# Another order of TensorE's matmuls between the two layers of a CIN kernel (f32, one Trainium2 core)

## The chip, the cores and the metric

The kernel runs on one core of one Trainium2 chip (trn2). The metric is the device time of one execution in microseconds; for a version of the kernel it is the median of several runs. A profile is one further execution, recorded by the hardware profiler, whose own time stands beside it. In the profile PE is TensorE (matmuls), PEld its weight loads, DVE VectorE, ACT ScalarE, POOL GpSimd and SP SyncE (here only DMA issues).

## The reference

Two layers of a compressed interaction network over x of shape 4096 rows x 32 fields x 16 embedding values, all in f32:

```python
def _cin_layer(out, x, W, b, gamma, beta):
    r, _, e = x.shape
    h = jnp.einsum('rne,rfe->rnfe', out, x).reshape(r, -1, e)
    h = jnp.einsum('rce,oc->roe', h, W) + b[None, :, None]
    return _batchnorm(h, gamma, beta)      # over rows and embedding values
h1 = _cin_layer(x, x, W1, b1, g1, beta1)
out, direct1 = (h1[:, :64], h1[:, 64:])
direct2 = _cin_layer(out, x, W2, b2, g2, beta2)
return jnp.concatenate([direct1, direct2], axis=1).sum(axis=-1)
```

Layer 1 has 128 output channels. The first 64 (here "kept") feed layer 2; the other 64 ("direct") are only normalized and summed. The batch norm needs the mean and variance of a channel over all 65,536 sites (row x embedding value), so layer 2 can't begin before the last kept channel of the last site is known.

## The kernel before

**Layer 1** goes over 128 tiles of 512 sites (`T`). DVE forms the products of pairs of fields as `z` (L365), PE multiplies them by W1: four matmuls per tile with a contraction of 128 rows (L397), and one with 32 rows for the field pairs at distance d = 16, whose products stand in `zr` for eight tiles at once (L358). ACT evicts each PSUM bank three times: for the statistics, for the kept half (to `h`, stored in DRAM) and for the direct half (`ed`). DVE's `bn_stats` collects the statistics.

**The last four tiles** (`ENDING`, k = 0 to 3) are done in column halves from L423 on, so that the kept channels of all four are ready first. A phase (`direct` = 0 for kept, 1 for direct) multiplies by only 64 columns of W1. Two tiles' halves stand in different column halves of the array and run side by side: tile k writes the half `(k + direct) % 2` of its own bank. Each bank thus takes a kept half in the first phase and a direct half, on the other 64 partitions, in the second. `begin_halves` (L438) issues the four d = 16 matmuls of a phase, one for each tile on its own 32 rows of the array; they open the accumulation in their banks. `add_halves` (L428) adds the main products of two tiles, four matmuls each, alternating between the tiles.

In the kept phase (L458 to L471) ACT evicts the two kept halves of a chunk of two tiles (L468), DVE takes their statistics (L470), and the chunk is stored. Then a short chain on DVE and ACT (`ScaleShift`, L474 to L479) makes the scale and shift of the 64 kept channels, and L484 makes `blocks` from them. A small matmul with `spread` (L502) spreads these to the layout that layer 2 multiplies in, DVE copies the result from PSUM to `keep` (L503).

In the direct phase (L494 to L516) PE's order is: the four d = 16 matmuls, the main products of tiles 0 and 1, the first main product of tiles 2 and 3, the spreading matmul, the other three main products of tiles 2 and 3. ACT evicts the direct halves of tiles 0 and 1 (L511) right after; those of tiles 2 and 3 are put off into layer 2 (`late_evictions`).

**Layer 2** goes over 64 chunks of 2 x 512 sites, each in four stages. In a stage ACT turns a loaded part of `h` into a factor `f` (L630, scaled and shifted by `keep`), DVE multiplies it with x into `zz` (L643 for the very first stage, in four parts, L638 for the others), POOL forms sums of these (L674, L677, L685), and PE multiplies by combinations of W2 (L669). The field products come in a scheme with fewer multiplications, hence the sums.

**What sets the order.** Nothing is planned by cost. From L423 on, every instruction of PE, DVE, ACT and POOL goes through `queue` (L226), which chains it behind the one before it on its engine: an engine's instructions start in the order in which the Python code makes them. Waits between engines follow from who writes and reads a tile. A matmul into a bank half that opens an accumulation waits until ACT has evicted what stood in that bank. All of these matmuls are recorded under L426 (where `matmul` issues them), all factors under L630 (where `act` does).

Of the kernel before, what the change touches and what calls it, by code (L numbers as in the profile page):

```python
# [68 lines left out]
def tile_cin(ctx: ExitStack, tc: tile.TileContext, xa, xb, xr, w1, w1m, w2, bn, out):  # L69
# [156 lines left out]
    def queue(engine, make):  # L226

        with tc.issue_after(lasts[engine].ins) if engine in lasts else nullcontext():
            lasts[engine] = make()
        return lasts[engine]  # L230
# [4 lines left out]
    begun = factors.tile([P, T], FP, tag="f", name="begun")  # L235
# [25 lines left out]
    with ExitStack() as one:  # L261
# [23 lines left out]
        w1_sb = wpool.tile([P, 6, P], FP, tag="w1", name="w1_sb")  # L285
# [62 lines left out]
        def leftovers(r):  # L348
            zr = rpool.tile([P, T], FP, tag="zr", name="zr")
            nc.vector.tensor_tensor(zr, r[:, :T], r[:, T:], ALU.mult)  # L350
            return zr
# [23 lines left out]
        for t in range(NT - ENDING):  # L375
# [5 lines left out]
            if s == 0 and t > 0:  # L381
                zr = leftovers(r)
# [5 lines left out]
            if t == 0:  # L388
                with tc.issue_after(product.ins):
                    zr = leftovers(r)  # L390
# [32 lines left out]
        half_of = (low, high)  # L423

        def matmul(ps, w, z, start, stop):
            queue("pe", lambda: nc.tensor.matmul(ps, w, z, start=start, stop=stop))  # L426

        def add_halves(banks, zs, direct, ks, ms):  # L428

            for m in ms:  # L430
                for k in ks:
                    matmul(
                        banks[k][half_of[(k + direct) % 2]],
                        w1_sb[:, m, half_of[direct]],
                        zs[k][:, m // 2, m % 2, :],
                        False,
                        m == 3,
                    )  # L438

        def begin_halves(banks, zr, direct):  # L440

            for k in range(ENDING):
                rows = slice(32 * k, 32 * (k + 1))
                to = banks[k][half_of[(k + direct) % 2]]
                matmul(to, w1_sb[rows, 5, half_of[direct]], zr[rows, :], True, False)

        zs = []
        for k in range(ENDING):
# [5 lines left out]
        with tc.issue_after(lasts["dve"].ins):  # L454
            for t in (ending - 2, ending - 1):
                evicted = finish(t)
        banks = [psum.tile([P, T], FP, tag="ps", name="ps") for _ in range(ENDING)]
        begin_halves(banks, zr, 0)  # L458
        for c in range(NC - ENDING // 2, NC):
            ks = tuple(2 * c + half - ending for half in range(2))  # L460
            add_halves(banks, zs, 0, ks, range(4))
            h = opool.tile([KEEP, 2 * T], FP, tag="h", name="kept")
            for half, k in enumerate(ks):
                at = half_of[half]
                to = h[:, half * T : (half + 1) * T]
                bias = (b1, b1_swapped)[half][at]
                with tc.issue_after(evicted.ins):
                    queue("act", lambda: nc.scalar.activation(to, banks[k][at], AF.Identity, bias=bias))  # L468
                stats = stats1.more[low, 2 * k : 2 * k + 2].rearrange("p a b -> p (a b)")
                queue("dve", lambda: nc.vector.bn_stats(stats, to))  # L470
            nc.scalar.dma_start(hs[c], h)  # L471
# [19 lines left out]
        keep_ps = factors.tile([P, 4, 2], FP, tag="f", name="keep_ps")  # L491
        keep = const.tile([P, 4, 2], FP, tag="keep", name="keep")

        begin_halves(banks, zr, 1)  # L494
        for c in range(NC - ENDING // 2, NC):
            eds[c] = epool.tile([P, T], FP, tag="ed", name="ed")
            ks = tuple(2 * c + half - ending for half in range(2))
            if c < NC - 1:
                add_halves(banks, zs, 1, ks, range(4))
            else:  # L500
                add_halves(banks, zs, 1, ks, range(1))
                matmul(keep_ps, spread, blocks, True, True)  # L502
                queue("dve", lambda: nc.vector.tensor_copy(keep, keep_ps))  # L503
                add_halves(banks, zs, 1, ks, range(1, 4))
            for half, k in enumerate(ks):
                at = half_of[1 - half]
                bias = (b1, b1_swapped)[half][at]
                to = eds[c][half_of[half]]

                def evict(to=to, at=at, bias=bias, k=k):  # L510
                    return nc.scalar.activation(to, banks[k][at], AF.Identity, bias=bias)  # L511

                if c < NC - 1:
                    queue("act", evict)
                else:
                    late_evictions.append(evict)  # L516

    direct = const.tile([P, 2], FP, tag="direct", name="direct")
# [463 lines left out]
```

## Time and profile before

| | us |
|---|---|
| median of 5 runs | 2092.37 |
| lowest and highest of them | 2091.89, 2095.96 |
| the profiled execution | 2093.71 |
| its span, first to last instruction | 2091.6 |
| granted PE clock over the span | 0.996 |
| first matmul of layer 1, of the kept phase, of the direct phase | 9.82, 475.05, 483.08 |
| spreading matmul | 492.26 |
| first matmul of layer 2, last one | 496.15, about 2074 |

The times in the lower rows are counted from the first instruction of the profiled execution. A row of the time line reads: start, duration, engine, line, operation, output<-inputs, shape, how many were merged; in brackets, how long the engine had been idle and what released it. PE's rows merge instructions that overlap, so a duration spans the whole group. One f32 matmul shows as two passes, each with its own weight load; so `x8` in a row of PE are four matmuls. `128*64` means a contraction of 128 rows and 64 output columns. An engine that waits at the head of its queue holds all that stands behind.

### The profile page before, as it was taken

The page shows a single profiled execution, that of the slowest core. Times are in us where ns is not written, and L with a number is a line of the kernel's source. Part 1 is how long each engine was busy: PE and PEld are TensorE (multiplying, and loading weights), DVE is VectorE, ACT ScalarE, POOL GpSimd, SP SyncE. Part 2 cuts the span into 40 slices and gives each one's busy share as a digit, 9 for nine tenths or more (in the row PEclk, how much of TensorE's full clock was granted, in tenths as well). Part 3 has the DMA queues.
Part 4 walks back from the last instruction along what each step waited for, and adds up shares of the span by engine and source line. Part 5 has one row for each costly group of instructions (what it writes and reads, how often), then busy time and mean ns, then how long its engine had stood idle before and what let it go on. Part 6 is the DMA issues. An engine that isn't in the chain of part 4 may idle for free.

```text
span 2091.6 us, 23628 instructions
## 1 busy us (share of the span) xinstructions
PE 2069.3 (99%) x8634; PEld 1029.6 (49%) x8634; DVE 1890.5 (90%) x1391; ACT 1007.9 (48%) x1594; POOL 1471.7 (70%) x453
## 2 busy tenths in 40 slices
PE   9999999999999999999999999999999999999996
PEld 3444444443443555555555555555555555555553
DVE  8998888887999999999999998999999989999996
ACT  4555555554454444444444445454444454444443
POOL 0000000003899999999999999999999999999995
PEclk9999999999999999999999999999999999999998
DMA  9999999996766687777676777766677777767751
GB/s 385 378 347 349 333 359 354 347 337 178 174 162 171 162 195 188 193 175 173 162 191 166 183 176 176 173 172 162 171 167 186 173 174 176 171 163 169 171 142 41
DMA packets 112020, 440.65 MB, mean 211 GB/s; under 512 B 13088, under 2 KB 13088, under 8 KB 103456
## 3 DMA queue, kind: packets, MB, share of 16 engines
q1 hardware_dynamic: 105456, 418.43, 73.2%
q10 hardware_dynamic: 6448, 20.72, 2.6%
q8 instruction: 67, 1.10, 0.2%
q14 instruction: 49, 0.40, 0.1%
HBM read 417.07 MB, written 22.02 MB: 210 GB/s over the span
## 4 chain that ended last, share of the span: by engine, by line
PE 94%; DVE 2%; POOL 1%; issue 1%; ACT 1%; DMA 1%; DVEq 0%; SPq 0%; ACTq 0%; POOLq 0%
PE x L669 72%; PE ps L397 21%; PE ps L358 2%; DVE zz L638 1%; POOL t L677 0%; DMA h<-kept 0%; POOL t L674 0%; PE ps L426 0%; DMA b<-in_xb 0%; ACT f L630 0%; DVE zz L643 0%; DVE e L633 0%; ACT both L630 0%; DVE z L365 0%; DVE d L912 0%
## 5 line engine op out<-in xcount | busy, mean ns | idle before, releaser
L669 PE MATMUL x<-zz,s_sb 128*64 128x512 f32 x2048 | 946.8, 592 | 1.0 <-PE ps L426 0.8
L669 PE MATMUL x<-zz,w_sb 128*64 128x512 f32 x2312 | 890.3, 593 | 0.0
L677 POOL TENSOR_TENSOR t<-zz,t 128x2048 f32<-128x2048 f32 x191 | 870.8, 4559 | 15.0
L669 PE MATMUL x<-t,s_sb 128*64 128x512 f32 x1528 | 694.2, 593 | 0.1
L630 ACT ACTIVATE f<-a,keep 128x512 f32<-128x512 f32 x512 | 398.1, 778 | 415.2 <-DVE zz L638 373.1
L638 DVE TENSOR_TENSOR zz<-f,b 128x2048 f32<-128x2048 f32 x255 | 580.6, 2277 | 0.1
L638 DVE TENSOR_TENSOR zz<-f,bx 128x2048 f32<-128x2048 f32 x255 | 579.8, 2274 | 0.0
L674 POOL TENSOR_TENSOR t<-zz 128x1024 f32<-128x1024 f32 x191 | 453.1, 2372 | 89.8 <-DVE zz L638 80.1
L685 POOL TENSOR_TENSOR th<-zz,th 128x1024 f32<-128x1024 f32 x64 | 151.9, 2374 | 490.7 <-DVE th L633 490.7
L397 PE MATMUL ps<-z,w_sb 128*128 128x512 f32 x992 | 434.3, 596 | 1.3 <-DVE z L365 1.3
L669 PEld LDWEIGHTS x<-zz,s_sb 128*64 128x64 f32 x2048 | 280.1, 137 | 227.1 <-issue 163.5
L669 PEld LDWEIGHTS x<-zz,w_sb 128*64 128x64 f32 x2312 | 306.8, 137 | 168.1 <-issue 88.6
L669 PE MATMUL x<-t,w_sb 128*64 128x512 f32 x764 | 360.9, 595 | 0.9 <-POOL t L677 0.9
L365 DVE TENSOR_TENSOR z<-a,b 128x2048 f32<-128x2048 f32 (+1 forms) x129 | 293.7, 2278 | 54.3 <-PE ps L397 43.8
L669 PEld LDWEIGHTS x<-t,s_sb 128*64 128x64 f32 x1528 | 206.6, 137 | 223.8 <-issue 182.0
L397 PEld LDWEIGHTS ps<-z,w_sb 128*128 128x128 f32 x992 | 186.2, 190 | 247.2 <-issue 239.1
L329 ACT ACTIVATE e<-ps,bn_sb 128x512 f32<-128x512 f32 x124 | 85.2, 687 | 224.2 <-PE ps L397 205.0
L630 ACT ACTIVATE u<-e,bn_sb 64x512 f32<-64x512 f32 x64 | 46.3, 723 | 218.9 <-DVE e L633 218.9
L669 PE MATMUL x<-th,s_sb 128*64 128x512 f32 x256 | 130.8, 592 | 0.0
L633 DVE TENSOR_TENSOR both<-both,x 128x512 f32<-128x512 f32 x64 | 44.0, 688 | 94.6 <-ACT both L630 94.6
L669 PEld LDWEIGHTS x<-t,w_sb 128*64 128x64 f32 x764 | 101.9, 137 | 54.3 <-issue 18.9
L669 PE MATMUL x<-zz,neg_sb 128*64 128x512 f32 x264 | 124.1, 592 | 0.0
(104 smaller groups left out, 1233.1 us busy)
## 6 DMA issues: line engine op xcount, KB each, us to landing
a<-h SPq DMA_DIRECT2D x256, 512.0 KB, 5.7
a<-in_xa SPq DMA_DIRECT2D x128, 512.0 KB, 6.4
b<-in_xb SPq DMA_DIRECT2D x128, 512.0 KB, 7.4
b<-in_xb SPq DMA_DIRECT2D x64, 1024.0 KB, 8.8
bx<-in_xb SPq DMA_DIRECT2D x64, 512.0 KB, 7.8
bx<-x SPq DMA_DIRECT2D x64, 512.0 KB, 9.4
h<-kept ACTq DMA_DIRECT2D x64, 256.0 KB, 5.6
r<-in_xr SPq DMA_DIRECT2D x16, 512.0 KB, 7.6
```

Source lines behind the costliest of these rows:

```text
L329: nc.scalar.activation(e, ps, AF.Identity, bias=b1)
L358: nc.tensor.matmul(pss[t + k], w1_sb[rows, 4 + t % GROUP // 4, :], zr[rows, :], start=not ended, stop=ended)
L365: return nc.vector.tensor_tensor(z[:, k], a.rearrange("p (a t) -> p a t", a=2)[:, k].unsqueeze(2).to_broadcast([P, n, 2, T]), b.rearrange( ...
L397: nc.tensor.matmul(pss[t], w1_sb[:, m, :], z[:, m // 2, m % 2, :], start=(t == m == 0), stop=(t > 0 and m == 3))
L630: return queue("act", lambda: nc.scalar.activation(to, source, AF.Identity, **scale_bias))
L633: return dve(lambda: nc.vector.tensor_tensor(to, x, y, ALU.add))
L638: dve(lambda: nc.vector.tensor_tensor(z, a, b.rearrange("p (k q) t -> p k q t", k=2), ALU.mult))
L669: queue("pe", lambda: nc.tensor.matmul(self.of[x], w, b, start=start, stop=stop))
L674: queue("pool", lambda: nc.gpsimd.tensor_tensor(t[:, 0], z[:, 1], z[:, 0], ALU.add))
L677: queue("pool", lambda: nc.gpsimd.tensor_tensor(t[:, 1:3], z[:, 2:4], twice, ALU.subtract))
L685: queue("pool", lambda: nc.gpsimd.tensor_tensor(t[:, 1:3, 0], z[:, 2:4, 1], twice, ALU.subtract))
```

## The change

Only the order of PE's matmuls in the direct phase changes, with the marks that open (`start`) and end (`stop`) the accumulation in each bank. Before, the d = 16 matmuls of all four tiles came first and opened it. Now the main products of tiles 0 and 1 come first and open their banks; then come the four d = 16 matmuls, which end the accumulation of tiles 0 and 1 and open that of tiles 2 and 3; then the spreading matmul; then all main products of tiles 2 and 3. The kept phase is as it was. `begin_halves` is now `add_leftovers_halves`.

```diff
-        def add_halves(banks, zs, direct, ks, ms):
-
-            for m in ms:
+        def add_halves(banks, zs, direct, ks, begun, ended):
+
+            for m in range(4):
                 for k in ks:
                     matmul(
                         banks[k][half_of[(k + direct) % 2]],
                         w1_sb[:, m, half_of[direct]],
                         zs[k][:, m // 2, m % 2, :],
-                        False,
-                        m == 3,
+                        m == 0 and not begun,
+                        m == 3 and ended,
                     )
 
-        def begin_halves(banks, zr, direct):
+        def add_leftovers_halves(banks, zr, direct, begun):
 
             for k in range(ENDING):
                 rows = slice(32 * k, 32 * (k + 1))
                 to = banks[k][half_of[(k + direct) % 2]]
-                matmul(to, w1_sb[rows, 5, half_of[direct]], zr[rows, :], True, False)
+                matmul(to, w1_sb[rows, 5, half_of[direct]], zr[rows, :], k not in begun, k in begun)
...
-        begin_halves(banks, zr, 0)
+        add_leftovers_halves(banks, zr, 0, ())
         for c in range(NC - ENDING // 2, NC):
             ks = tuple(2 * c + half - ending for half in range(2))
-            add_halves(banks, zs, 0, ks, range(4))
+            add_halves(banks, zs, 0, ks, True, True)
...
-        begin_halves(banks, zr, 1)
         for c in range(NC - ENDING // 2, NC):
             eds[c] = epool.tile([P, T], FP, tag="ed", name="ed")
             ks = tuple(2 * c + half - ending for half in range(2))
             if c < NC - 1:
-                add_halves(banks, zs, 1, ks, range(4))
-            else:
-                add_halves(banks, zs, 1, ks, range(1))
+
+                add_halves(banks, zs, 1, ks, False, False)
+                add_leftovers_halves(banks, zr, 1, ks)
                 matmul(keep_ps, spread, blocks, True, True)
                 queue("dve", lambda: nc.vector.tensor_copy(keep, keep_ps))
-                add_halves(banks, zs, 1, ks, range(1, 4))
+            else:
+                add_halves(banks, zs, 1, ks, True, True)
```

## The prediction

> **What bounds the kernel now.** I read the page first, then the busy time by stages, then the rows of TensorE (PE) around the change, then those of ScalarE (ACT) and VectorE (DVE) there.
>
> ```profile
> span 2091.6 us, 23628 instructions
> PE 2069.3 (99%) x8634; PEld 1029.6 (49%) x8634; DVE 1890.5 (90%) x1391; ACT 1007.9 (48%) x1594; POOL 1471.7 (70%) x453
> ```
>
> PE is busy for 99% of the span. Time is saved either by shortening PE's work or by taking out one of its few stalls. The stages show where those are (columns: stretch, its length, busy time of PE, PEld, DVE, ACT and POOL, then granted clock, DMA share, GB/s):
>
> ```profile
> 482.68:486.09 3.41, 3.10 (x12) 0.56 (x8) 1.59 (x3) 1.36 (x2) 0.00 (x0) 1.00 0.60 215
> 486.09:489.51 3.42, 3.42 (x9) 1.01 (x10) 1.38 (x8) 0.59 (x2) 0.00 (x0) 0.50 0.35 77
> ...
> 492.92:496.33 3.41, 2.63 (x14) 0.79 (x12) 2.64 (x3) 1.45 (x2) 0.00 (x0) 1.00 0.19 30
> 496.33:572.45 76.12, 74.86 (x338) 31.45 (x336) 71.48 (x51) 35.51 (x58) 62.32 (x20) 1.00 0.70 170
> 572.45:2074.00 1501.55, 1501.55 (x6962) 793.46 (x6962) 1379.77 (x935) 719.32 (x1141) 1405.75 (x427) 1.00 0.70 169
> ```
>
> The reader is to see three things. From 572.45 to 2074 PE never stops: whatever moves the start of layer 2 moves the end. Between 496.33 and 572.45 PE lacks only 1.26 us. And from 486.09 to 489.51 its clock was granted at 0.50, after a window in which it was "busy" 3.10 of 3.41 us, but mostly with passes of 32 rows. The seam between the layers is therefore the place. Its PE rows (start, duration; one f32 matmul is two passes):
>
> ```profile
> 475.05 1.09 PE L426 MATMUL ps<-zr,w_sb 32*64 32x512 f32 x8
> ...
> 476.06 7.09 PE L426 MATMUL ps<-z,w_sb 128*64 128x512 f32 x32
> ...
> 484.46 1.79 PE L426 MATMUL ps<-zr,w_sb 32*64 32x512 f32 x4 [0.31 <-ACT kept L468]
> ...
> 486.18 6.14 PE L426 MATMUL ps<-z,w_sb 128*64 128x512 f32 x20
> ...
> 492.26 0.39 PE L426 MATMUL keep_ps<-blocks,spread 64*128 64x8 f32 x2
> ```
>
> The eight d = 16 passes of the kept phase take 1.01 us until the next work starts (475.05 to 476.06). The same eight in the direct phase take from 483.08 to 486.18, 3.10 us, since the last two tiles' matmuls wait for ACT to evict the kept halves of their banks. Who waits for whom after that:
>
> ```profile
> 484.43 0.68 ACT L468 ACTIVATE kept<-ps,b_swapped 64x512 f32<-64x512 f32 x1
> ...
> 487.68 0.16 DVE L484 TENSOR_TENSOR blocks<-block,ss 64x8 f32<-64x8 f32 x1
> ...
> 491.50 0.68 ACT L511 ACTIVATE ed<-ps,bn_sb 64x512 f32<-64x512 f32 x1 [4.44 <-PE ps L426]
> 492.21 0.68 ACT L511 ACTIVATE ed<-ps,b_swapped 64x512 f32<-64x512 f32 x1
> ...
> 492.68 0.17 DVE L503 COPY keep<-keep_ps 128x8 f32<-128x8 f32 x1 [4.84 <-PE keep_ps L426]
> ...
> 492.88 1.48 ACT L630 ACTIVATE f<-a,keep 128x512 f32<-128x512 f32 x2
> ...
> 493.69 1.23 DVE L643 TENSOR_TENSOR zz<-f,b 128x1024 f32<-128x1024 f32 x1 [0.85 <-ACT f L630]
> ```
>
> The factors that open layer 2 (`blocks`) are ready at 487.84, but their spreading matmul stands in PE's queue behind ten slots of main products and starts at 492.26. The first `f` needs `keep` (copied by 492.85) and ACT, which evicts two direct halves until 492.89. DVE's first `zz` starts at 493.69, the first matmul of layer 2 at 496.15.
>
> **The change part by part.** Nothing is added or removed on any engine: the same 16 main matmuls, four d = 16 matmuls and one spreading matmul, with other start and stop marks. The queues of ACT, DVE, POOL and SP keep their order, and no DMA issue moves past another. So the sum is one of waiting.
>
> *Main products first.* Two tiles' halves run side by side, so 16 passes are 8 slots. A slot is 0.43 us at full clock (7.09 us for 16 slots with the drain). The slot after the last kept one is due at 482.98 (the last issues at 482.55). Their banks 0 and 1 were evicted by 481.14, so nothing holds them. 482.98 + 8 x 0.43 = 486.42.
>
> *Then the four d = 16 matmuls.* Banks 2 and 3 are evicted by 485.11 (484.43 + 0.68), 1.3 us before they are asked for: the wait goes. They cost what they cost in the kept phase: 0.09 for the change of rows (such gaps lie at each change in layer 1), 1.09 to their end: 486.51 to 487.60. What hid nothing before hides now: the eviction lies beside main products.
>
> *Evictions, then f.* ACT starts the first direct eviction 0.04 after PE's end (491.46 to 491.50), the second 0.71 later, and `f` 0.67 after that: 487.64, 488.35, **489.02**.
>
> *The spreading matmul.* PE is free for it near 487.55 and waits for `blocks` until 487.84 + 0.05 (an ACT end to the waiting weight load: 484.41 to 484.46) = 487.89, a new wait of about 0.35 us. Queued behind it are the last 8 slots. It takes 0.39, the copy 0.04 + 0.17, so `keep` stands at 488.49 and `f` could start at 488.52. ACT is free only at 489.02, so the evictions, not the factors, end last. The bounds of this step: 488.52 if the evictions run earlier than I think, and later than 489.02 only if `blocks` slips by over 0.5 us. I take 489.02, from the nearer rows.
>
> *The last 8 slots* restart 0.31 after the spreading matmul (492.26 to 492.57): 488.20 + 3.44 + 0.17 drain = 491.8. With `f` 3.86 earlier the first matmul of layer 2 is due at 496.15 - 3.86 = 492.29, so they hide behind `f` and `zz` with 0.5 us to spare. The late evictions of banks 2 and 3 come on ACT at 499.21 - 3.86 = 495.35, long after.
>
> **The sum:** 492.88 - 489.02 = **3.86 us**. About 2.0 of it is the wait in the d = 16 block (3.10 against 1.01 plus 0.09), 1.7 the half clock: four slots of 0.86 in place of 0.43 after 486.18, which come only because the 32-row block fills a window. All that follows hangs on `f`, so it moves as one. By the profiled execution (2093.71 us, of which 2091.6 span) that makes 2089.85. That execution lies 1.34 above the median of the five runs, 2092.37. If the ordinary runs pay what the trace shows, their median goes to **2088.5**.
>
> [...]
>
> **The rivals.**
>
> *A, the gate was open in ordinary runs.* [...] For: the profiled run is 1.34 over the median, close to 1.7. Against: four of the five runs lie within 0.8 us, no two groups 1.7 apart. Then `keep` in before comes four half slots earlier (4 x 0.43 = 1.7) and the gain is 3.86 - 1.7 = 2.2: **2090.2**.
>
> *B, the start is earlier and the gain is lost before 572.* POOL's sums release PE at 572.45, and there PE lacks about 1 us; the loads of the second chunk wait for `f` too. Against: POOL's first sum waits for `zz`, and SP's loads from 494.39 for `f`, so both move along. If something fixed in time holds them, 0 to 1.3 us is left: about **2091.5**.
>
> *C, slower: the gate closes at the start of layer 2.* From 486.5 to 488.2 PE now has 32-row passes, a wait and 8-column passes. One closed window costs 3.41 / 2 = 1.7 on PE; the first is nearly covered (0.5 spare at 491.8, 1.26 up to 572). If the gate kept closing, three windows eat the gain (5.1 - 1.26 = 3.86) and six make it 5.1 us slower: **2097.5**. Against: a window with 2.63 of 3.41 us busy (492.92 to 496.33) kept its clock at 1.00 in the next.
>
> *D, the factors end last.* If `f` starts at 488.52, the gain is 4.4: **2088.0**.
>
> **How the numbers follow.** The forecast, 2088.5, has 0.50 (alone 2088.0 to 2089.0); A 0.32; B 0.07; C 0.03; D 0.08. A difference of 0.2% is about what a measurement of this kernel can tell from no change; that is 4.2 us, so the forecast lies just within it. Of the forecast's 0.50 I give 0.16 to beyond 4.2 us, by the scatter of medians, and D is all beyond: faster 0.24, slower 0.03 (C), within 0.73. The range takes in D less 0.3 of scatter and A plus 0.4: 2087.7 to 2090.6; it leaves out B, C and the tails.
>
> **What would show it.** After: d = 16 passes starting near 486.5 without an ACT wait; a clock of 1.00 from 486 to 490; `keep` by 488.5; first `f` near 489.0, straight after two evictions; first L669 near 492.3; PE without a gap from about 568.6. I am wrong if ordinary runs of before show no half clock (A), if `f` waits for `keep` rather than ACT, or if L669 starts early and PE's idle time up to 572 grows (B).

## The result and the profile after

The changed kernel took 2089.93 us in the median of 21 runs (2089.56 to 2091.1). The kernel before took 2094.1 us in the median of 39 runs on the same chips (2091.73 to 2097.95). The ratio is 0.9981, with a 95% interval of 0.9975 to 0.9987: about 4.0 us less, 0.19%, just inside the 0.2% that I had set as the bound (the two medians lie 4.2 us apart). The five runs of before that the prediction started from lay low among the 39: their median was 2092.37.

The profiled execution of the changed kernel took 2090.14 us, with a span of 2088.1, 3.6 less than before's. The time line around the seam (columns as above; PE, ACT and DVE):

```profile
476.04 10.52 PE L426 MATMUL ps<-z,w_sb 128*64 128x512 f32 x48
...
484.57 0.68 ACT L468 ACTIVATE kept<-ps,bn_sb 64x512 f32<-64x512 f32 x1 [3.45 <-DMA h<-kept]
...
486.49 1.09 PE L426 MATMUL ps<-zr,w_sb 32*64 32x512 f32 x8
...
488.53 0.16 DVE L484 TENSOR_TENSOR blocks<-block,ss 64x8 f32<-64x8 f32 x1
488.64 0.68 ACT L511 ACTIVATE ed<-ps,b_swapped 64x512 f32<-64x512 f32 x1
488.74 0.39 PE L426 MATMUL keep_ps<-blocks,spread 64*128 64x8 f32 x2 [1.16 <-DVE blocks L484]
...
489.36 1.48 ACT L630 ACTIVATE f<-a,keep 128x512 f32<-128x512 f32 x2
```

The reader is to see the kept phase run straight into the main products of tiles 0 and 1 (48 passes in one row), and the eight d = 16 passes done in 1.09 us without a wait. What was not forecast is the bracket of the second row: ACT waits 3.45 us for a *store* (`h<-kept`) before it can evict the kept halves of banks 2 and 3. The *landing* of a store is the end of its piece in the chain below, which frees its buffer. So `blocks` ends at 488.69 in place of 487.84, PE waits 1.2 us for it, and `keep` and `f` follow. The stages of the changed kernel (columns as above) show no half clock, and about the same 1.26 us of PE time missing up to 572:

```profile
486.09:489.51 3.42, 2.26 (x16) 0.70 (x14) 2.36 (x10) 2.10 (x5) 0.00 (x0) 1.00 0.48 132
489.51:492.92 3.41, 3.41 (x18) 1.09 (x16) 2.74 (x3) 1.34 (x2) 0.00 (x0) 1.00 0.11 36
...
496.33:572.45 76.12, 74.85 (x340) 30.87 (x338) 71.70 (x51) 35.61 (x59) 64.06 (x20) 1.00 0.72 173
```

The chain that ended last says the same (start, length, what): in the changed kernel it runs from the store's landing through the statistics to `f`.

```profile
476.42 8.07 DMA h<-kept
...
484.57 0.69 ACT kept L468
...
488.53 0.17 DVE blocks L484
...
489.36 0.79 ACT f L630
```

In the chain of before the same piece stood too, and I had read past it:

```profile
476.44 7.20 DMA h<-kept
...
483.73 0.69 ACT kept L468
...
484.46 7.06 PE ps L426 x20
```

The evictions write into `h`, a pool of two buffers. The one for the last chunk (63) is free only when the store of chunk 61 has landed.

### The profile page after: what moved, and what is told of

It is laid out like the page before. It is cut to its first block, busy times and chain, and to the rows that moved or that the text cites. A ratio compares the mean times of both kernels' runs of the same rounds, so it can differ in the third digit from the quotient of the medians.

```text
span 2088.1 us, 23629 instructions
## 1 busy us (share of the span) xinstructions
PE 2067.1 (99%) x8634; PEld 1017.0 (49%) x8634; DVE 1890.7 (91%) x1391; ACT 1007.9 (48%) x1594; POOL 1471.7 (70%) x453
## 4 chain that ended last, share of the span: by engine, by line
PE 95%; DVE 2%; POOL 1%; issue 1%; ACT 1%; DMA 0%; DVEq 0%; ACTq 0%; POOLq 0%
PE x L669 72%; PE ps L397 21%; PE ps L358 2%; DVE zz L638 1%; POOL t L677 0%; PE begun L237 0%; DMA h<-kept 0%; POOL t L674 0%; ACT f L630 0%; DVE zz L643 0%; DVE e L633 0%; ACT both L630 0%; DVE d L912 0%; ACT unread L568 0%; ACT u L630 0%
## 5 line engine op out<-in xcount | busy, mean ns | idle before, releaser
L669 PE MATMUL x<-zz,s_sb 128*64 128x512 f32 x2048 | 946.3, 592 | 0.3 <-DVE zz L638 0.3
L669 PE MATMUL x<-zz,w_sb 128*64 128x512 f32 x2312 | 889.7, 593 | 0.0
L669 PE MATMUL x<-t,s_sb 128*64 128x512 f32 x1528 | 694.4, 594 | 0.1
L669 PEld LDWEIGHTS x<-zz,s_sb 128*64 128x64 f32 x2048 | 280.1, 137 | 231.8 <-issue 161.6
L669 PEld LDWEIGHTS x<-zz,w_sb 128*64 128x64 f32 x2312 | 306.1, 137 | 162.1 <-issue 77.7
L669 PE MATMUL x<-t,w_sb 128*64 128x512 f32 x764 | 360.9, 595 | 0.9 <-POOL t L677 0.9
L669 PEld LDWEIGHTS x<-t,s_sb 128*64 128x64 f32 x1528 | 206.5, 137 | 237.5 <-issue 186.9
L669 PE MATMUL x<-th,s_sb 128*64 128x512 f32 x256 | 130.8, 592 | 0.0
L669 PEld LDWEIGHTS x<-t,w_sb 128*64 128x64 f32 x764 | 101.9, 137 | 49.6 <-issue 13.4
L669 PE MATMUL x<-zz,neg_sb 128*64 128x512 f32 x264 | 124.1, 592 | 0.0
```

What stands on the lines that cost most here:

```text
L669: queue("pe", lambda: nc.tensor.matmul(self.of[x], w, b, start=start, stop=stop))
```

## The experiments

Three theories stood against each other. **S**: the order of the matmuls and the closed gate make the gain, in ordinary runs too. **A**: the gate is open in ordinary runs. **L**, formed on the profile after: the landing of the store sets the seam in both kernels, and differs from run to run. A stretch in which the profile grants PE's clock at 0.50 is called a closed window; "the gate is closed" says no more than that. In before's closed window at the seam (486.09 to 489.51) pairs of weight loads of the main products start 0.85 to 0.86 us apart, behind it 0.42 to 0.43. Each comparison below is with the kernel before on the same chip.

One thing is to be kept in mind for small differences. The time of a run is longer than its span, by 2.07 to 2.11 us on average in before, the changed kernel, e3, e4, e7 and e11, but by only 1.71 to 1.73 in e2, e5, e6, e8 and e10. Where this comes from is open. Between a version of one group and one of the other, about 0.35 us of a difference in time thus lies outside the span, where the time line shows nothing.

**e1**, the kernel before, unchanged, for the span and granted clock of each run.

> The kernel before, unchanged, for the span and the granted clock of each of its runs. Theory S (the forecast): the d = 16 block of the direct phase waits for evictions and its low use of the array closes PE's clock gate in ordinary runs too, so most runs have a lower mean clock than the changed kernel's 0.997, and the median lies about 3.9 us over its 2089.9. Theory A (the gate is open in ordinary runs): clocks of 0.997 in most runs, and only the runs some 1.7 us longer have less. Theory L (the landing of the store of the kept chunk before last, for which ACT's second pair of kept evictions waits, differs from run to run and sets the time): runs spread over several us at one and the same clock.

Measured: 2094.4 us (2092.39 to 2097.42, 11 runs) beside 2094.49 of 35 more; ratio 0.9997 (0.9988 to 1.0005). The 46 runs by their mean clock: 12 runs at 0.997 took 2091.71 to 2093.14, 21 at 0.996 took 2092.4 to 2097.12, 13 at 0.995 or less took 2095.91 to 2099.11. A closed window of 3.41 us at half clock is worth 0.0008 of this mean (3.41 / 2 in 2091 us), and the third digit separates the ends only: of the profiles here, those at 0.997 have no closed window before PE's last matmul, those at 0.995 (e3, e8) have two, and 0.996 stands for none (e4), one (before) and two (e1). So A holds for at least the quarter at 0.997, closed windows for the 13 at 0.995 or less, and the 21 between stay open. No single account holds for all. Its profile shows two closings, at 11.33 (start of layer 1, all later work 2.7 us late) and at the seam, as its stages show:

```profile
7.92:11.33 3.41, 1.01 (x4) 0.30 (x3) 1.88 (x2) 0.20 (x1) 0.59 (x1) 1.00 1.02 407
11.33:14.75 3.42, 3.42 (x6) 1.34 (x5) 3.03 (x6) 0.00 (x0) 0.00 (x0) 0.50 1.03 420
485.78:489.20 3.42, 2.51 (x10) 0.55 (x8) 1.41 (x3) 1.37 (x2) 0.00 (x0) 1.00 0.97 289
489.20:492.61 3.41, 3.41 (x9) 1.01 (x10) 1.57 (x8) 0.59 (x2) 0.00 (x0) 0.50 0.37 96
```

**e2**, before with a buffer of its own for the last kept chunk.

```diff
-            h = opool.tile([KEEP, 2 * T], FP, tag="h", name="kept")
+            h = (wpool if c == NC - 1 else opool).tile([KEEP, 2 * T], FP, tag="h", name="kept")
```

> The kernel before, with a buffer of its own for the last kept chunk, so that its evictions no longer wait for a store to land. Theory L: evictions of banks 2 and 3 start 0.5 us earlier in the profile of before (483.73 to 483.19) and more in runs with a later landing; the median falls by 1 to 2.5 us against before and the spread of the runs shrinks to about 1 us. Theories S and A, by which the order of the matmuls alone costs the time: the median falls by no more than 0.5 us and the spread stays at several us.

Measured: 2091.73 us (2091.12 to 2092.15, 11 runs), ratio 0.9986 (0.9978 to 0.9995). The median falls by 2.8, the spread from about 7 us to 1.0, and the clock is 0.996 or 0.997 in every run. By the spans it falls by 2.4, from 2092.4 to 2090.0. That is L, whose forecast was 1 to 2.5; S and A had said no more than 0.5. With the wait cut short the gate stays open too (clock 1.00 from 479.28 to 492.94); its d = 16 block, for all it still waits for, takes 2.54 us to the next work:

```profile
483.29 2.61 PE L426 MATMUL ps<-zr,w_sb 32*64 32x512 f32 x8
483.39 0.68 ACT L468 ACTIVATE kept<-ps,bn_sb 64x512 f32<-64x512 f32 x1 [2.04 <-PE ps L426]
...
485.83 4.51 PE L426 MATMUL ps<-z,w_sb 128*64 128x512 f32 x20
```

The eviction now waits for PE, not for the store.

**e3**, before with the spreading matmul alone moved ahead, by one pair of main products.

```diff
-                add_halves(banks, zs, 1, ks, range(1))
                 matmul(keep_ps, spread, blocks, True, True)
                 queue("dve", lambda: nc.vector.tensor_copy(keep, keep_ps))
-                add_halves(banks, zs, 1, ks, range(1, 4))
+                add_halves(banks, zs, 1, ks, range(4))
```

> The kernel before, with the spreading matmul alone put one pair of main products (0.86 us) earlier, ahead of the main products of tiles 2 and 3; the d = 16 block stays first. Theory S: the first f is held by the two direct evictions of tiles 0 and 1, which end at 492.89 as before, so nothing is gained: 0 to 0.1 us. The rival that the place of the spreading matmul is what costs: 0.9 us faster.

Measured: 2093.16 us (2091.56 to 2097.46, 12 runs), ratio 0.9993 (0.9985 to 1.0002). The times don't tell 0 from 0.9 us. The profile does: `keep` ends at 495.87, 0.8 before `f` (496.68), which follows the second direct eviction, begun at 496.09. The place of the spreading matmul alone gains nothing at `f`.

**e4**, the changed kernel with the spreading matmul put back behind the first main products of tiles 2 and 3.

```diff
...
                 add_leftovers_halves(banks, zr, 1, ks)
-                matmul(keep_ps, spread, blocks, True, True)
-                queue("dve", lambda: nc.vector.tensor_copy(keep, keep_ps))
             else:
-                add_halves(banks, zs, 1, ks, True, True)
+                add_halves(banks, zs, 1, ks, True, True, range(1))
+                matmul(keep_ps, spread, blocks, True, True)
+                queue("dve", lambda: nc.vector.tensor_copy(keep, keep_ps))
+                add_halves(banks, zs, 1, ks, True, True, range(1, 4))
```

> The changed kernel, with the spreading matmul put back behind the first main products of tiles 2 and 3; only the d = 16 block is moved against before. Theory S: blocks is ready about 488 to 488.7, while PE has two slots to do in that time, so the spreading matmul starts at 488.5 to 488.8 and f at 489.1 to 489.4: the same time as the changed kernel within 0.4 us, about 2090. The rival that the place of the spreading matmul makes the gain: some 1 us or more slower than the changed kernel, 2091 or above.

Measured: 2090.3 us (2089.57 to 2094.75, 11 runs), ratio 0.9981 (0.9972 to 0.9989), as the change itself. In its profile the spreading matmul starts at 488.86 without a wait, and `f` at 489.49. So the gain comes from moving the d = 16 block behind main products; by e3 and e4 the place of the spreading matmul adds little or nothing. Three of its runs lie between 2092.5 and 2094.8; their cause is open.

**e5**, the changed kernel with the buffer of e2.

> The changed kernel, with a buffer of its own for the last kept chunk as in e2. Theory L carried on: in the profile of the changed kernel the store's landing (484.49) now sets blocks, keep and f (489.36); without that wait blocks is ready 0.9 to 1.4 us earlier, f is held by the two direct evictions and starts at about 488.95: 0.3 to 0.5 us faster than the changed kernel, about 2089.5, runs within 0.8 us of each other. If PE's order alone set f: no difference.

Measured: 2089.5 us (2089.05 to 2090.21, 9 runs), ratio 0.9976 (0.9966 to 0.9986). By the time and the narrow spread this is what L expects: 0.4 below the changed kernel's 2089.93 and 1.0 below the 2090.45 of e9. But 0.35 of that lies outside the span; the median spans are 2087.8 here, 2087.9 in the changed kernel and 2088.3 in e9. So the buffer is worth 0.1 to 0.5 us there. Now `blocks` ends at 487.69 and `keep` at 488.51, and `f` starts at 489.31 behind the evictions. Against e2 this is the change with no landing and no closed gate in either profile (clock 0.997 in both): 2091.73 - 2089.50 = 2.2 us, though on another chip. In the two profiles `f` stands only 1.6 us earlier (490.90 to 489.31), or 1.8 counted from the start of the kept phase; 0.5 of the 2.2 lies behind PE's last matmul.

**e6**, e5 with ACT's first two factors ahead of the two direct evictions.

```diff
...
                 if c < NC - 1:
-                    queue("act", evict)
+                    first_evictions.append(evict)
...
                 f2 = factor(raw[i], i, 1)
+                for evict in first_evictions:
+                    queue("act", evict)
                 for q in range(2):
```

> As e5, and on ACT the first two factors f go ahead of the two direct evictions of tiles 0 and 1. By the forecast's claim that the evictions, not the factors, end last: keep stands at about 488.1 and f starts there, 0.8 us earlier than in e5, and PE's last main products (ending near 491.4) just meet the first matmul of layer 2: about 2088.7. If keep ends last anyway: the same as e5; if the later evictions hold the first matmuls of layer 2 (two of their banks are needed there): slower than e5.

Measured: 2088.61 us (2088.41 to 2089.02, 7 runs), ratio 0.9969 (0.9958 to 0.9981): the fastest version here, 0.9 below e5, as expected. In its time line PE waits for nothing in the seam any more (ACT still waits for `keep`):

```profile
486.47 1.09 PE L427 MATMUL ps<-zr,w_sb 32*64 32x512 f32 x8
...
487.10 0.16 DVE L485 TENSOR_TENSOR blocks<-block,ss 64x8 f32<-64x8 f32 x1
487.49 0.39 PE L427 MATMUL keep_ps<-blocks,spread 64*128 64x8 f32 x2
487.80 3.65 PE L427 MATMUL ps<-z,w_sb 128*64 128x512 f32 x16
...
491.38 0.61 PE L670 MATMUL x<-zz,s_sb 128*64 128x512 f32 x1
```

`blocks` (to 487.26) is ready before PE is, and the last main products (to 491.45) meet the first matmul of layer 2.

**e7**, before with four passes of 128 rows and 128 columns in the wait of the d = 16 block. They write a bank that nobody reads.

```diff
                 matmul(to, w1_sb[rows, 5, half_of[direct]], zr[rows, :], True, False)
+                if direct == k == 1:
+                    filler = factors.tile([P, T], FP, tag="f", name="filler")
+                    for _ in range(2):
+                        matmul(filler, w1_sb[:, 0, :], zs[0][:, 0, 0, :], True, True)
```

> The kernel before, with two matmuls of 128 rows and 128 columns (four passes, 1.7 us, into a bank that nobody reads) between the d = 16 matmuls of tiles 1 and 2 of the direct phase, where PE waits. If the low use of the array in that wait closes the gate and this costs 1.7 us: no half clock after the block, lowest runs up to 0.6 us slower, since the filler outlasts the wait, and the median 1 us faster. If the gate has nothing to do with it: a median slower by 0.6 us, or no change where the landing is late.

Measured: 2093.15 us (2092.71 to 2094.01, 11 runs), ratio 0.9996 (0.9987 to 1.0005). The lowest run is 0.5 above the lowest of before on that chip (2092.22), the median 1.3 below its 2094.43, no run has a clock under 0.996, and its profile shows none at 0.50 up to PE's last matmul. The filler lowers the median as the gate theory expects, but the ratio's interval takes in no change, so that the time falls isn't shown. What is shown is the clock: of before's 26 runs of 2092 to 2098 us on that chip three lie at 0.995, and before's profile has a closed window where this one has none. The way to `f` is 1.6 us shorter for it (table below).

**e8**, before with `BEGIN = 8` (warm-up matmuls) in place of 6.

> The kernel before, with 8 warm-up matmuls at the start in place of 6, which lie in the wait for the first loads. In e1 and e3 the profile shows the gate closed at 11.3 to 12.2 us, at the start of layer 1, and all that follows 2.7 to 3.5 us later than in before. If that closing makes the highest runs of before (2096 to 2098): they go, with the runs at a granted clock of 0.995, and the median falls by 0.5 to 1.5 us; what is left lies between 2091.7 and 2095. If not: the same spread and the same median.

Measured: 2095.9 us (2093.15 to 2097.72, 11 runs), ratio 1.0005 (0.9996 to 1.0014). A miss: the highest runs stay, and the median lies 1.5 above the 2094.43 of before there, which the interval doesn't tell from no change. The start of its profile has no closing; its seam has one that lasts two windows:

```profile
482.63:486.04 3.41, 2.21 (x9) 0.38 (x6) 0.48 (x1) 1.17 (x2) 0.00 (x0) 1.00 0.98 318
486.04:489.45 3.41, 3.41 (x8) 0.81 (x8) 2.49 (x10) 0.78 (x3) 0.00 (x0) 0.50 0.55 159
489.45:492.87 3.42, 3.42 (x10) 0.95 (x8) 0.00 (x0) 0.00 (x0) 0.00 (x0) 0.50 0.00 0
```

So the seam alone can make a run of 2096.5 (the profiled one); what share the start has in the highest runs stays open.

**e9**, the changed kernel again, beside e10 and e11.

> The changed kernel, unchanged, beside the before on this chip, to set e5, e6 and e11 against. By e2 and e5 the change is worth 2.2 us (2091.73 to 2089.50) where the store's landing costs nothing and the gate stays open; the rest up to 4.2 between the medians is what landing and gate cost before alone. So runs of the changed kernel should lie at 2089.5 to 2091, with no run at a granted clock of 0.995, and those of before spread from 2091.7 to 2098. If the narrow spread of the first 21 runs was chance, some runs here lie at 2092 to 2095.

Measured: 2090.45 us (2089.67 to 2092.46, 11 runs), ratio 0.9983 (0.9975 to 0.9992), 4.0 below the 2094.45 of before there. No run at 0.995; one at 2092.46, so its spread is wider than the first 21 runs told. Its profile has an earlier landing than the first one of this kernel (about 484.22), and here `f` comes straight behind the second eviction, not behind `keep`:

```profile
488.67 0.68 ACT L511 ACTIVATE ed<-ps,b_swapped 64x512 f32<-64x512 f32 x1
488.90 0.17 DVE L502 COPY keep<-keep_ps 128x8 f32<-128x8 f32 x1 [0.48 <-PE keep_ps L426]
489.25 1.48 ACT L630 ACTIVATE f<-a,keep 128x512 f32<-128x512 f32 x2
```

So which of the two ends last changes from run to run with the landing.

**e10**, before with the two `xs` loads issued in the middle of layer 1.

```diff
             if c % DIFF == 2:
-                with tc.issue_after(loads[-1].ins):
+                with tc.issue_after((lasts["dve"] if c == 2 else loads[-1]).ins):
```

> The kernel before, with two 512 KB loads of layer 2 (xs, issued by SP at 468.3 to 471.8, just ahead of the store of chunk 61 at 476.4) issued in the middle of layer 1 instead, where their buffer is already free. If these loads make the store land late (7.2 us in the profile of before), it lands within about 5.6 us, the median of all 64 such stores, so about 482; the kept evictions of banks 2 and 3 then start right behind PE, and the runs look like e2: median near 2091.7, spread about 1 us. If other traffic makes it land late: no change, 2094 with the same spread.

Measured: 2091.85 us (2091.26 to 2093.95, 11 runs), ratio 0.9989 (0.9980 to 0.9998). The time is near the one expected (2.6 below before's, of which 0.35 lies outside the span), but not by the way expected: in its profile the store still takes 7.18 us to land. The kept evictions and the d = 16 block lie as in before's profile (483.16 to 486.23, there 483.08 to 486.18). Yet no window closes, the clock is 1.00 in both stretches below. That these are the windows here is my estimate, from the steps of 3.4133 us in the last section; no closed window of e10 shows it. Each takes in main products as well:

```profile
481.55:484.96 3.41, 3.12 (x13) 0.67 (x10) 0.85 (x2) 1.15 (x2) 0.00 (x0) 1.00 0.54 161
484.96:488.38 3.42, 3.42 (x14) 0.96 (x14) 2.51 (x10) 0.81 (x3) 0.00 (x0) 1.00 0.35 77
```

In before one window, 482.68 to 486.09, held nearly the whole block and the next was closed. The closed window goes with 1.65 us more on the way from the landing to `f` (9.24 there, 7.59 here; table below). Whether these loads make the late landings of other runs stays open.

**e11**, the factors first as in e6, without the buffer.

> The changed kernel, with the first two factors ahead of the two direct evictions on ACT as in e6, but without the buffer of e5. In the profile of the changed kernel keep ends at 489.33 and f starts at 489.36, so the evictions (487.94 to 489.32) cost nothing where the store lands that late: 0 to 0.1 us in such runs, up to 0.9 where it lands early; median 2089.3 to 2089.9, above the 2088.6 of e6. If the evictions alone held f in most runs: about 2088.7, as e6.

Measured: 2091.03 us (2089.39 to 2092.35, 11 runs), ratio 0.9986 (0.9977 to 0.9994), no better than e9, and a miss: 2089.3 to 2089.9 was expected. The profile fell on a very late landing (486.56), which holds even the d = 16 block (2.11 us) and PE for 1.66 us at the spreading matmul. Where the store ends last, the order on ACT is worth nothing, and the runs show no gain from it alone; e6 needs both edits.

**One account of them all.** In each profile where the store's landing held the kept eviction, the way from landing to first `f` follows from the order and from the closed windows (the landing is the end of the store's piece in the chain; for e3, e4, e7 and e9, whose chains leave it out, it is put 0.08 before the eviction, as in the others):

| kernel | store landed | first f | between | closed windows |
|---|---|---|---|---|
| before | 483.64 | 492.88 | 9.24 | 1 |
| e1 (before again) | 486.94 | 496.18 | 9.24 | 1 |
| e3 (spreading matmul alone) | 487.50 | 496.68 | 9.18 | 1 |
| e8 | 484.76 | 495.56 | 10.80 | 2 |
| e7 | 485.63 | 493.23 | 7.60 | 0 |
| e10 | 483.70 | 491.29 | 7.59 | 0 |
| changed | 484.49 | 489.36 | 4.87 | 0 |
| e11 | 486.56 | 491.44 | 4.88 | 0 |
| e9 (changed again) | 484.22 | 489.25 | 5.03 | 0 |
| e4 (block alone) | 484.39 | 489.49 | 5.10 | 0 |

In e9 the evictions hold `f`, as shown above; in e4 PE reaches the spreading matmul only at 488.86, 0.27 after `blocks` ends. The change makes this way 2.7 us shorter with the gate open, 4.4 with one closed window, 5.9 with two. Where neither landing nor gate costs anything it is worth 2.2 by the medians and 1.6 to 1.8 at `f` (e2 to e5). The 4.0 to 4.2 between the medians is a mixture of these; in what shares isn't shown.

## Why the prediction was right, and where it was off

- **The wait in the d = 16 block goes, 2.0 us.** Right: 3.10 became 1.09 (486.49 to 487.58), without an ACT wait, and e4 shows that this move is the gain. What I called ACT's eviction was, one step further back, the store for which ACT waited. I took its end, 485.11, as fixed.
- **The half clock goes, 1.7 us.** Right in the profiles: no closed window at the seam in the changed kernel's two (clock 1.00 from 482.68 to 496.33 in the first, 0.997 over the span of e9), and e7 and e10 show the old order without one. Wrong as a constant: it is 0, 1.6 or 3.2 us of the way to `f`, depending on the run. That it comes only because the 32-row block fills a window was my guess from one row, and no run shows it as a rule: the clock fell after windows in which PE showed 3.10 (before), 2.51 (e1) and 2.21 us (e8) of 3.41 busy, largely with 32-row passes, but also, at the start of e1, after one with 1.01 us in four passes (7.92 to 11.33). The closed stretches at the seam lasted 3.41 to 3.42 (e1, before) and 6.83 us (e8).
- **The evictions, not the factors, end last (489.02).** Wrong in the first profile of the changed kernel: `f` started at 489.36, behind `keep`, which I had named as a sign of being wrong. I had named the bound too (if `blocks` slips by over 0.5 us); it slipped by 0.85, the later landing. In e9's profile of the same kernel, and with the landing out of the way (e5), the step holds, and e6 gains the rest by turning that order round.
- **The new wait at the spreading matmul, 0.35 us.** Mis-sized: 1.2, for the same reason. It cost what lay behind it nothing, since `f` waited for the same thing.
- **All that follows moves as one.** Right: first L669 at 492.63 (forecast 492.29), PE without a gap from 568.95 (568.6), and 1.26 against 1.27 us missing between 496.33 and 572.45. Rival B falls.
- **The base of the sum.** This made the point 2088.5 too low by 1.4 us. I took 3.86, which holds one closed window, from a median of five runs of which four, at 2091.89 to 2092.66, lie by their times in the band of the runs at 0.997 (2091.71 to 2093.14); their own clock isn't on record. So the time measured is rival A's rather than the forecast's own (2092.37 - 2.2 = 2090.2, measured 2089.93); it lies in the range because the range took A in. That the larger sample gives the same by the forecast's sum (2094.1 - 3.86 = 2090.2) is in part luck: its median holds landings that the sum took as fixed, and runs with no, one and two closed windows.
- **Rival C** did not appear in any profile of the new order. **Rival D** needed the factors early and ACT free: e6 is that case, by two further edits.

## What to carry to other kernels

When an engine's wait is named in a profile, follow it one step further: here PE waited for ACT, and ACT for a store that had to land before a buffer of two came free. Put dense work of the same engine under such a wait. Here that hid the wait (the block took 1.09 us in place of 3.10) and most of its spread from run to run (2089.56 to 2091.1 in place of 2091.73 to 2097.95), and no profile of the new order has a closed window at the seam (none in the table for four of them; clock 1.00 from 482.68 to 496.33 in e6, 0.997 over the span of e5). Before taking a gain from a median, ask whether the runs of that median paid what the profiled run paid.

## What the runs showed of the hardware

- PE's granted clock fell to 0.50 after windows that the profile shows as mostly busy, largely with 32-row passes: 3.10 (before), 2.51 (e1) and 2.21 us (e8) of 3.41. Counting only 128-row passes, by an estimate from the rows' starts, these windows held about 0 (e1, 485.78 to 489.20), 0.4 (before, 482.68 to 486.09) and 0.6 us of them (e8, 482.63 to 486.04). A busy share alone doesn't tell the outcome: in the changed kernel the clock stayed at 1.00 after a stretch with 2.42 us busy (485.16 to 488.57), of which about 1.2 with 128-row passes. Nor does the count of 128-row passes: at the start of e1 the clock fell after 1.01 us in four passes (7.92 to 11.33), none of them of 32 rows by the kernel's order (in before's profile the first such pass comes at 13.43). What makes it fall isn't shown.
- In e1 the falls to 0.50 at 11.33 and 489.20 lie 477.87 us apart, in before those at 486.09 and 2076.70 lie 1590.61 apart: 140 and 466 times 3.4133 us. The closed stretches at the seam are one or two times as long. That windows of this length lie in the other profiles too, and where, is an estimate from these; by it the stretch of the changed kernel above ends 465 of them before its fall at 2075.76.
- Whether before pays differs from run to run: e10 and before have the same landing (7.18 and 7.20 us) and block (483.16 to 486.23, 483.08 to 486.18), and only before has a closed window. That the place of the windows makes this difference is an estimate. A second closed window followed in e8, where the block still filled 2.1 us of the first (486.04 to 488.18).
- The landing of one and the same 256 KB store, near a DMA share of 1 (1.04 and 1.02 in before from 475.85 to 482.68), took 7.2 to 8.2 us from issue in these profiles (7.18 in e10, 7.20 in before, 7.81 in e1, 7.84 in e8, 8.07 in the changed kernel, 8.19 in e11). In e11 it was issued late as well, at 478.37, 1.4 us after the eviction that fills it ended (476.95); the chain shows a load of 12.65 us just ahead of the issue.
- That loads in front hold a store's landing isn't shown: in e10 two of them, issued at 468.3 to 471.8 in before, are issued in the middle of layer 1, and the store took 7.18 us, beside 7.20 in before.
